# First image's attention: VectorE and ScalarE in written order, with the folding's work dealt out unit by unit

## The chip, the cores and the metric

The kernel runs on one core of a Trainium2 chip. The core has a matrix engine (TensorE, PE in the profile, its weight loads PEld), a vector engine (VectorE, DVE), an engine for activation functions (ScalarE, ACT), a general one (GpSimd, POOL) and an engine that issues transfers (SyncE, SP), each with its own in-order queue; they wait for one another through semaphores. The metric is the device time of one execution in microseconds, and the median of several executions is compared.

## The reference

Two layers follow each other on eight images of 512 channels and 32 x 32 positions.

```python
# layer 0, per image: group norm, q/k/v, each fake-quantized over ALL images, 8 heads of 64 channels
h = group_norm(xf, gn_w, gn_b)
qkv = einsum('oc,bct->bot', qkv_w, h) + qkv_b
q = fake_quant(q); k = fake_quant(k); v = fake_quant(v)
w = softmax(einsum('bct,bcs->bts', q * scale, k * scale))
a = einsum('bts,bcs->bct', w, v)
x = xf + einsum('oc,bct->bot', proj_w, a) + proj_b
# layer 1, per image: group norm, one head of 512 channels, no quantization
t = group_norm(x, gn_w, gn_b)
out = softmax((t wq + bq)(t wk + bk)^T / sqrt(C)) (t wv + bv)
x = x + (out wp + bp)
```

`fake_quant` needs the smallest and largest value of q, of k and of v over the whole batch, so no attention of layer 0 can start before all q, k and v exist.

## The kernel before, in words

**Stages.** The first stage normalizes all images, computes q, k and v, collects their extremes and stores them to DRAM (`q_d`, `k_d`, `v_d`). From about 585 us the scales are known and layer 0's attention begins. It is a generator, `attention()`, that is advanced four units at a time; with the second image on, layer 1 of the image before runs between its steps ("planned" part: `others()`).

**Units.** A unit `u` is one (image `b`, head pair `j`, half `hf` of the queries, key block `s` of eight). `scores(u)` puts two 64-row matmuls into one of two score buffers in PSUM (`st`); ScalarE takes the exponential into `pt` (four buffers) or, for every fourth unit of the first image (`plain`), into `aside`. `split(u)` makes a 16-bit high part of `pt` (a cast: on GpSimd for `s % 4 == 2`, on VectorE for `s == 5` before planning starts, on ScalarE otherwise) and VectorE subtracts to get the low part (`two<-pt,two`). `over_keys` multiplies both parts with v (`av`), `totals` with ones (`sm`). Eight units are a half, sixteen a pair, 64 an image. In one advance at unit u, the scores run up to nine units ahead and the splits with them. `finish` copies `av` and `sm` out of PSUM and starts the reciprocals of the row sums: two small loads (`apart`), `spread` on VectorE, a store and a broadcast load, then `divide`.

**Quantizing.** `load_pair(b, j, u)` is called sixteen units before a pair is used. It fetches the raw q and k (two buffers `raw`, which v shares), and `quants(i)` lists the steps `quant` and `quant2` for q, k, v (and `whole`, a 32-bit copy of part of v, in the first image).

**Folding.** Layer 1 uses folded weights, the product of two weight matrices (`wa` for q and k, `wm` for v and the output). `fold()` is a generator of 32 products and some small steps; nine steps are taken before attention starts, and then one in every second unit of the first image.

**What sets the order.** PE is always in written order (`mm` ties each matmul to the last one). VectorE and ScalarE are objects of the class `InOrder`. With `InOrder.planned` set (during the first image of stage one, and from the second image's first layer 1 on) each of their instructions is tied to the one before. Between, as in the first image's attention, a scheduler below the kernel chooses their order when the program is built. In that time the kernel has a list `dealt` of (unit, name, work): `deal(u)`, called by `split(u)`, takes the first entry whose unit has come, one per split, and `settle(name)` takes all of a name at once, as `scores` does with "qk" at the first unit of a pair and the main loop with "qv" when the pair's values are used. In the planned part `deal` isn't called, work goes through `dve.later` with times of the kernel's own planner, and `settle` still empties the list. Nearly all instructions go through line 91 (`call` in `InOrder`) or line 208 (`mm`), so the profile is read by the names of tiles.

Of the kernel before, what the change touches and what calls it, by code (L numbers as in the profile page):

```python
# [21 lines left out]
CC = C // P  # L22
# [36 lines left out]
def attn_pair_kernel(  # L59
# [12 lines left out]
    class InOrder:  # L72
# [1 line left out]

        planned = False

        def __init__(self, engine):
            self.engine, self.last, self.t, self.chores = engine, None, 0.0, []  # L80
# [6 lines left out]
        def __getattr__(self, name):  # L87
            op = getattr(self.engine, name)

            def call(*args, **kw):  # L90
                ins = self.latest = op(*args, **kw).ins  # L91
                if InOrder.planned:
                    if name == "dma_start":
                        self.t = max(self.t, pe.t) + 0.5
                    if self.last is not None:
                        tc.add_manual_dep(ins, self.last.name, IN_ORDER, reason="order")
                    self.last = ins
                elif self.last is not None:
                    tc.add_manual_dep(ins, self.last.name, IN_ORDER, reason="order")

            return call
# [204 lines left out]
    with ExitStack() as fast:  # L306
# [611 lines left out]
        def deal(u):  # L918
            i = next((i for i, (at, *_) in enumerate(dealt) if at <= u), None)
            if i is not None:  # L920
                dealt.pop(i)[2]()

        def settle(what):
            while True:
# [8 lines left out]
        def load_pair(b, j, u=None):  # L933

            nm = f"{b}_{j}"
            raws = []

            def fetch(i, src):
                if (b, j, i) == (0, 0, 2):
                    raw = aop.tile([P, NH, 512], F32, tag="ao", name="raw_first").rearrange(  # L940
                        "p h n -> p (h n)"
                    )
                else:
                    raw = raw_p.tile([P, T], F32, tag="raw", name=f"raw_{nm}_{i}")
                nc.sync.dma_start(
                    raw if i < 2 else raw.rearrange("p (t d) -> p t d", t=NT), src
                )
                raws.append(raw)

            def whole(raw, _, i):  # L950
                quant2(raw.rearrange("p (t d) -> p t d", t=NT)[:, 3::4, :], vfs[j], i)

            fetch(0, q_d[b][j])
            fetch(1, k_d[b][j])
            qt = qkp.tile([P, T], BF, tag="q", name=f"q_{nm}")
            kt = qkp.tile([P, T], BF, tag="k", name=f"k_{nm}")
            vt = qkp.tile([P, NT, P], F16, tag="v", name=f"v_{nm}")
            todo = (qt, kt, vt.rearrange("p t d -> p (t d)"))

            if b == 0:  # L960
                vfs[j] = xp.tile([P, 2, 256], F32, tag="x", name=f"vf_{nm}")[:, :, 0:P]

            def quants(i):
                for step in (quant, quant2, *([whole] if i == 2 and b == 0 else [])):
                    name, work = "qk" if i < 2 else "qv", lambda step=step: step(raws[i], todo[i], i)
                    if u is None or InOrder.planned:
                        dve.later(name, 0.7, work, pe.t + 12.0, 45.0)
                    else:
                        dealt.append((u + (10 if i < 2 else 18), name, work))

            def fetch_v():
                if len(raws) == 2:
                    fetch(2, v_d[b][:, :, bass.ts(j, P)])
                quants(2)

            if (b, j) == (0, 0):
                fetch(2, v_d[b][:, :, bass.ts(j, P)])
            quants(0)
            quants(1)
            if u is None or InOrder.planned:  # L980
                dve.later("qk", 0.0, fetch_v)
            else:
                dealt.append((u + 10, "qk", fetch_v))
            return qt, kt, vt


        def attention():
# [13 lines left out]
            def scores(u):  # L1001
                b, j, hf, s = units[u]
                if hf == 0 and s == 0:
                    settle("qk")
                nm = f"{b}_{j}_{hf}"
                qt, kt, _ = pairs[b, j]
                st = pair_ps(f"st_{nm}_{s}")
                if b == 0 and u % 2 == 1:
                    next(folding, None)
                awaits(st_free[-2])  # L1010
                for i, r in enumerate(HALF):
                    mm(
                        st[:, i, :], lhsT=kt[r, bass.ts(s, P)],
                        rhs=qt[r, bass.ts(hf, 512)], start=True, stop=True,
                    )
                if u >= 4:
                    need(u - 4)
                if plain(b, s):
                    pt = aside[:, u // 4 % 3].rearrange("p (i k) n -> p i (k n)", i=2)
                else:  # L1020
                    pt = ptp.tile([P, 2, 512], F32, tag="p", name=f"pt_{nm}_{s}")
                there = act.do(
                    1.12, lambda: act.activation(pt, st, AF.Exp, scale=esc),
                    max(pe.t + 0.25, ready.get(u - 4, 0.0) + 0.1),
                )
                st_free.append(there)
                pts[u] = pt, there
# [80 lines left out]
            def finish(b, j, hf, u):  # L1108
# [30 lines left out]
                def spread():  # L1139
                    r = rcs[:, n * 16 : (n + 1) * 16]  # L1140
                    dve.tensor_add(r, apart[:, 0, :], apart[:, 1, :])
                    dve.reciprocal(r, r)
                    nc.sync.dma_start(rs_d[n].rearrange("r (p k) -> (r p) k", k=16), r)
                    for i, r in enumerate(HALF):
                        nc.sync.dma_start(
                            rs[r], rs_d[n][2 * i : 2 * i + 2, :].partition_broadcast(CH)
                        )
                    if InOrder.planned:
                        dve.later("ao", elements(1100), divide, dve.t + 7.0, 20.0)
                    else:  # L1150
                        dealt.append((u + 17, "ao", divide))

                if InOrder.planned:
                    dve.later("ao", 0.4, spread, pe.t + 5.0, 8.0)
                else:
                    dealt.append((u + 10, "ao", spread))

            for u in (0, 2, 4):
                for i in (u, u + 1):
# [542 lines left out]
        def fold():  # L1702
# [16 lines left out]
            def through(i):  # L1719
                w, _, col = ((NQ1, NK1, V_BQ), (NV1, WP1, V_BV))[i]  # L1720
                z = small.tile([P, CC], F32, tag="z", name=f"z{i}")
                for e in range(CC):
                    dve.tensor_tensor_reduce(
                        room, wn[w][:, e, :], row, 1.0, 0.0, ALU.mult, ALU.add,
                        accum_out=z[:, e : e + 1],
                    )
                dve.tensor_add(z, z, vec[:, col : col + CC])
                widen(wide[:, i], z)

            for i, (rows, lw, rw) in enumerate(((wa_rows, NQ1, NK1), (wm_rows, NV1, WP1))):  # L1730
                for e in range(CC):
                    ps = bank(f"fold_{lw}_{e}")
                    for d in range(CC):
                        mm(
                            ps, lhsT=wn[lw][:, d, bass.ts(e, P)], rhs=wn[rw][:, d, :],
                            start=(d == 0), stop=(d == CC - 1),
                        )
                        if d + 1 < CC:
                            yield
                    act.copy(rows(e), ps.rearrange("p (a n) -> p a n", a=2))  # L1740
                    if e == CC - 1:
                        through(i)
                    yield
                dst, w = ((gb, NK1), (ob, WP1))[i]
                by_channel, _ = weigh(
                    bank, room, lambda e, w=w: wn[w][:, e, :], wide[:, i], f"f{i}"
# [3 lines left out]
                if i == 0:  # L1750
                    dve.tensor_copy(dst, tot)
                    a11, a12, a21, a22, s1, s2, s4 = (wa[:, i] for i in range(7))
                    tt(s1, a21, a22, ALU.add)
                    tt(s2, s1, a11, ALU.subtract)
                    tt(a21, a11, a21, ALU.subtract)
                    tt(s4, a12, s2, ALU.subtract)
                    yield
                    load_wp(0, nc.sync.dma_start)
                    load_x2(0, nc.sync.dma_start)
                else:  # L1760
                    dve.tensor_add(dst, tot, vec[:, V_BP : V_BP + CC])
            (m11, m12), (m21, m22), (v1, v2), (v3, v4) = ([t[:, i] for i in range(2)] for t in wm)
            tt(v1, m11, m12, ALU.subtract)
            tt(v2, m22, v1, ALU.subtract)
            tt(v3, m22, m12, ALU.add)
            tt(v4, m21, v2, ALU.subtract)
            for t, dst in zip(wm, wm_d):
                nc.sync.dma_start(dst, t)

        def check_sums():  # L1770

# [45 lines left out]
        folding = fold()  # L1817
        for _ in range(9):
            next(folding)
        while done < 1:  # L1820
            advance()
        for _ in folding:
# [1 line left out]

        for _ in range(LEAD):
            advance()
        for e in (dve, act):
            e.t = pe.t
        InOrder.planned = True
# [367 lines left out]
```

## Time and profile before

| | |
|---|---|
| median of three runs | 2587.91 us (2587.77 to 2590.59) |
| profiled execution | 2593.63 us, span 2591.8 us |
| first exponential of the first image | 591.34 us |
| first exponential of the second image | 701.39 us |
| first projection matmul (planned part) | 725.53 us |
| PE busy between 591.34 and 701.39 (110.05) | 101.61 us |
| DVE, ACT busy there | 97.84, 100.55 us |

A line of a timeline has the start, the time taken, the engine, the line, the operation, the tiles written and read, the number of instructions merged, and in brackets the idle time before it with what ended it. A line of a table by stretch has the stretch, its length, the busy time and number of instructions of PE, PEld, DVE, ACT and POOL, the granted PE clock (1.00 is full), and the share and speed of the DMA engines. The profiled execution is one run of its own; its times are compared with those of another profiled execution, and differences are put onto the median.

### The profile page before, as it was taken

How to read it: one execution, taken by the hardware profiler on the slowest of the kernel's cores; microseconds unless marked ns; L12 is line 12 of the kernel's file. 1: busy time of each engine (PE TensorE's matmuls, PEld its weight loads, DVE VectorE, ACT ScalarE, POOL GpSimd, SP SyncE). 2: the span in 40 equal slices, each digit the busy share in tenths (PEclk: the TensorE clock that was granted, in tenths of full speed). 3: DMA queues.
4: the chain of work that ended last, by engine and by line, in shares of the span. 5: the costliest groups of instructions: out<-in, count | busy, mean ns of one | idle time of the engine just before them, and what ended most of it. 6: DMA issues, size and time to landing. Idle time of an engine off the chain costs nothing.

```text
span 2591.8 us, 38710 instructions
## 1 busy us (share of the span) xinstructions
PE 2530.8 (98%) x15670; PEld 1756.9 (68%) x15670; DVE 1905.4 (74%) x2748; ACT 1358.8 (52%) x1696; POOL 195.6 (8%) x153
## 2 busy tenths in 40 slices
PE   7999999999889999999999999999999999999998
PEld 4788888873237765775677577757756775777787
DVE  6788777669867877777877787778777777775544
ACT  3222222218856675665566566747665665664121
POOL 0000000002210001000100010010001000100000
PEclk9899999999999999999999999999999999999999
DMA  4343333334311232223212331232232123212211
GB/s 168 130 146 136 114 120 121 130 124 137 115 50 54 62 115 98 62 79 111 86 58 73 121 99 58 95 112 65 79 107 99 46 79 122 83 54 82 86 37 39
DMA packets 156013, 243.09 MB, mean 94 GB/s; under 512 B 26544, under 2 KB 93104, under 8 KB 154288
## 3 DMA queue, kind: packets, MB, share of 16 engines
q1 hardware_dynamic: 125264, 182.81, 21.2%
q10 hardware_dynamic: 30560, 57.71, 6.5%
q8 instruction: 125, 2.05, 0.3%
q14 instruction: 64, 0.52, 0.1%
HBM read 153.64 MB, written 86.28 MB: 93 GB/s over the span
## 4 chain that ended last, share of the span: by engine, by line
PE 65%; DVE 3%; ACT 2%; issue 1%; DMA 1%; POOL 0%; ACTq 0%; SPq 0%; DVEq 0%
PE s L208 15%; PE o L208 14%; PE pj L208 9%; PE v2ps L208 7%; PE av L208 7%; PE g L208 6%; PE st L208 4%; PE sm L208 3%; ACT pt L91 1%; DVE acc L91 1%; DVE two L91 1%; DVE h L91 0%; DMA out_dram<-x 0%; DVE kept_u L91 0%; DVE p L91 0%
## 5 line engine op out<-in xcount | busy, mean ns | idle before, releaser
L91 ACT ACTIVATE pt<-st,esc 128x1024 f32<-128x1024 f32 x496 | 528.1, 1114 | 350.6 <-PE st L208 327.2
L91 DVE TENSOR_TENSOR two<-pt,two 128x1024 f16<-128x1024 f32 x496 | 603.9, 1233 | 131.0 <-POOL two L1047 107.3
L91 ACT CAST two<-pt 128x1024 f16<-128x1024 f32 x358 | 362.3, 1055 | 5.3 <-ACT p L91 5.1
L1047 POOL CAST two<-pt 128x1024 f16<-128x1024 f32 x128 | 173.2, 1353 | 1533.2 <-PE sm L208 768.5
L208 PE MATMUL av<-two,v 128*32 128x512 f16 x3968 | 245.8, 382 | 0.7 <-ACT ao L91 0.7
L208 PE MATMUL s<-g,h 128*128 128x256 f32 x1024 | 233.5, 381 | 0.0
L208 PE MATMUL pj<-ao,wp 128*128 128x512 f32 x512 | 223.6, 595 | 0.0
L208 PEld LDWEIGHTS s<-g,h 128*128 128x128 f32 x1024 | 193.4, 190 | 30.5 <-issue 4.3
L91 ACT ACTIVATE u_ring<-qkps,qkbt 128x512 f32<-128x512 f32 x89 | 61.0, 685 | 253.1 <-PE qkps L208 238.3
L208 PE MATMUL st<-q,k 64*128 64x512 bf16 x1024 | 166.6, 384 | 21.6 <-ACT pt L91 16.4
L208 PEld LDWEIGHTS <-v 128*32 128x32 f16 x3968 | 91.9, 96 | 134.4 <-issue 61.9
L208 PE MATMUL s<-g,sums 128*128 128x256 f32 x768 | 178.6, 382 | 0.2 <-DVE p L91 0.2
L208 PEld LDWEIGHTS pj<-ao,wp 128*128 128x128 f32 x512 | 96.3, 190 | 121.1 <-issue 110.9
L208 PE MATMUL o<-p,v 128*128 128x256 f32 x768 | 175.2, 382 | 1.0 <-DVE p L91 1.0
L208 PEld LDWEIGHTS o<-p,v 128*128 128x128 f32 x768 | 144.6, 190 | 26.8 <-issue 5.7
L208 PEld LDWEIGHTS s<-g,sums 128*128 128x128 f32 x768 | 144.8, 190 | 24.2 <-issue 4.1
L208 PEld LDWEIGHTS <-k 64*128 64x128 bf16 x1024 | 35.8, 94 | 159.8 <-issue 158.2
L208 PE MATMUL sm<-two,ones 128*32 128x512 f16 x1984 | 136.8, 381 | 0.0
L208 PE MATMUL qkps<-half,w_low 128*128 128x512 f32 x480 | 132.6, 399 | 1.9 <-DVE half L91 1.9
L208 PE MATMUL qkps<-half,w_high 128*128 128x512 f32 x480 | 134.4, 403 | 0.0
L208 PE MATMUL qkps<-half,w_mix 128*128 128x512 f32 x480 | 132.6, 399 | 0.6 <-DVE half L91 0.6
L208 PE MATMUL g<-h,wa 128*128 128x256 f32 x512 | 120.9, 385 | 1.8 <-DVE h L91 1.8
(221 smaller groups left out, 3832.1 us busy)
## 6 DMA issues: line engine op xcount, KB each, us to landing
rs<-rs_d SPq DMA_DIRECT2D x76, 256.0 KB
x<-in_x_dram SPq DMA_DIRECT2D x32, 512.0 KB
q_d<-wa SPq DMA_DIRECT2D x32, 512.0 KB
k_d<-wa SPq DMA_DIRECT2D x32, 512.0 KB
v_d<-v_ring SPq DMA_DIRECT2D x32, 512.0 KB
raw<-q_d SPq DMA_DIRECT2D x32, 512.0 KB
raw<-k_d SPq DMA_DIRECT2D x32, 512.0 KB
x_d<-h SPq DMA_DIRECT2D x64, 256.0 KB
```

The costliest lines, as they stand in the source:

```text
L91: ins = self.latest = op(*args, **kw).ins
L208: ins = nc.tensor.matmul(ps, lhsT=lhsT, rhs=rhs, **kw).ins
L1047: copy(two[:, 0], pt)
```

## The change

While the first image's attention is written, VectorE and ScalarE are now tied to the written order (`strict`, set after the first nine folding steps). With no scheduler to move work about, the other work of these engines is spread by hand through `dealt`: the row sums of folding (`through`, now started at the first product instead of the last), the sums for `wa` and `wm` and the stores of `wm` become entries that are taken one per split; q's steps are due at 12 and 13 units after the call of `load_pair`, k's at 14 and 15, v's at 19 and on (before: 10, 10 and 18); v's load follows q's second step directly (before: an entry of its own behind k); a pair's reciprocals are due at 12 instead of 10 units, its division at 20 instead of 17. Folding takes three steps in eight units instead of four, and goes on into the second image's first units.

```diff
-                if InOrder.planned:
                     if name == "dma_start":
                         self.t = max(self.t, pe.t) + 0.5
+                if InOrder.planned or InOrder.strict:
                     if self.last is not None:
                         tc.add_manual_dep(ins, self.last.name, IN_ORDER, reason="order")
...
         def deal(u):
             i = next((i for i, (at, *_) in enumerate(dealt) if at <= u), None)
             if i is not None:
                 dealt.pop(i)[2]()
+                if dealt[i : i + 1] and dealt[i][2].__name__ == "fetch_v":
+                    dealt.pop(i)[2]()
...
             def quants(i):
-                for step in (quant, quant2, *([whole] if i == 2 and b == 0 else [])):
+                for n, step in enumerate((quant, quant2, *([whole] if i == 2 and b == 0 else []))):
...
-                        dealt.append((u + (10 if i < 2 else 18), name, work))
+                        dealt.append((u + (12, 14, 19)[i] + n, name, work))
+                        if (i, n) == (0, 1):
+                            dealt.append((u + 13, "qk", fetch_v))
...
-            else:
-                dealt.append((u + 10, "qk", fetch_v))
...
-                if b == 0 and u % 2 == 1:
+                if u % 8 in (1, 4, 6):
                     next(folding, None)
...
-                        dealt.append((u + 17, "ao", divide))
+                        dealt.append((u + 20, "ao", divide))
...
-                    dealt.append((u + 10, "ao", spread))
+                    dealt.append((u + 12, "ao", spread))
...
                 for e in range(CC):
-                    dve.tensor_tensor_reduce(
+                    dealt.append((0, "fold", lambda e=e: dve.tensor_tensor_reduce(
...
-                dve.tensor_add(z, z, vec[:, col : col + CC])
-                widen(wide[:, i], z)
+                def last():
+                    dve.tensor_add(z, z, vec[:, col : col + CC])
+                    widen(wide[:, i], z)
+
+                dealt.append((0, "fold", last))
...
-                    if e == CC - 1:
+                    if e == 0:
                         through(i)
                     yield
+                settle("fold")
...
-                    tt(s1, a21, a22, ALU.add)
-                    tt(s2, s1, a11, ALU.subtract)
-                    tt(a21, a11, a21, ALU.subtract)
-                    tt(s4, a12, s2, ALU.subtract)
+                    for args in (
+                        (s1, a21, a22, ALU.add), (s2, s1, a11, ALU.subtract),
+                        (a21, a11, a21, ALU.subtract), (s4, a12, s2, ALU.subtract),
+                    ):
+                        dealt.append((0, "wa", lambda args=args: tt(*args)))
...
-            for t, dst in zip(wm, wm_d):
-                nc.sync.dma_start(dst, t)
+            def keep():
+                for t, dst in zip(wm, wm_d):
+                    nc.sync.dma_start(dst, t)
+
+            dealt.append((0, "wm", keep))
...
             next(folding)
+        InOrder.strict = True
         while done < 1:
             advance()
...
         for _ in range(LEAD):
             advance()
+        settle("wa")
+        settle("wm")
         for e in (dve, act):
             e.t = pe.t
         InOrder.planned = True
```

The four sums for `wm` become entries in the same way as those for `wa`.

## The prediction

> **What bounds the kernel now.** I read the page first, then busy time by stretch, the waits of the first image's attention, and there the instructions in order of time on TensorE (PE), ScalarE (ACT) and VectorE (DVE). The profiled execution took 2593.63 us (its span 2591.8, about 1.8 around it); the median of the runs is 2587.91, so I work out a difference on the trace and add it to the median. 0.2% is 5.2 us, about what a measurement of this kernel can tell from no change.
>
> ```profile
> PE 2530.8 (98%) x15670; PEld 1756.9 (68%) x15670; DVE 1905.4 (74%) x2748; ACT 1358.8 (52%) x1696; POOL 195.6 (8%) x153
> ```
>
> PE is 98% busy and runs its instructions in their written order, so the end moves by what PE waits, wherever it waits. I count units u = 0, 1, ...: one block of scores, one exponential on ACT each; eight are a half, sixteen a head pair, 64 the first image. Stretches of the first image (busy us of PE, weight loads, DVE, ACT, POOL, then the granted clock):
>
> ```profile
> 610.00:620.00 10.00, 10.00 (x100) 3.54 (x100) 9.96 (x11) 9.62 (x12) 1.81 (x2) 1.00 0.32 122
> ...
> 650.00:660.00 10.00, 8.21 (x72) 2.61 (x64) 7.00 (x10) 6.36 (x9) 1.44 (x2) 0.91 0.50 155
> ...
> 690.00:700.00 10.00, 8.20 (x104) 2.73 (x100) 8.64 (x10) 9.71 (x12) 1.55 (x1) 1.00 0.26 80
> ```
>
> While folding lasts (to about 683) PE is full, ACT has slack; afterwards ACT is full and PE idles a fifth. DVE is nearly full in the first row: three engines close to balance. The exponentials of units 8, 16 and 64, found by counting ACT's list:
>
> ```profile
> 603.60 1.11 ACT L91 ACTIVATE pt<-st,esc 128x1024 f32<-128x1024 f32 x1 [0.21 <-PE st L208]
> ...
> 617.25 1.11 ACT L91 ACTIVATE pt<-st,esc 128x1024 f32<-128x1024 f32 x1 [0.16 <-PE st L208]
> ...
> 701.39 1.17 ACT L91 ACTIVATE pt<-st,esc 128x1024 f32<-128x1024 f32 x1
> ```
>
> A half in the folding part takes 13.65 us; units 8 to 64 take 97.8 (13.97 a half, one DMA wait around 655 included).
>
> **Two rules weighed.** The Trainium skill, "SBUF — State Buffer", section "Who interferes with whom": a DVE instruction with two SBUF inputs and a GpSimd one that reads SBUF block each other. The trace agrees: POOL's cast at 629.16 ran inside the first subtraction below, which took 2.06 us against 1.21; I charge 0.84 per POOL cast.
>
> ```profile
> 629.68 2.06 DVE L91 TENSOR_TENSOR two<-pt,two 128x1024 f16<-128x1024 f32 x1
> 631.66 0.68 DVE L91 CAST two<-pt 128x1024 f16<-128x1024 f32 x1
> 632.52 1.21 DVE L91 TENSOR_TENSOR two<-pt,two 128x1024 f16<-128x1024 f32 x1
> 633.66 0.74 DVE L91 TENSOR_SCALAR raw<-raw,rcp 128x1024 f32<-128x1024 f32 x1
> ```
>
> "TensorE: Matmul & The Clock Gate", section "What's actually happening", has the clock halve after an idle window of about 3.4 us. Here a 1.79 us wait already did it: sixteen matmuls took 1.90 us instead of 1.05. I go by the trace: a PE wait of several us is followed by up to about 3.2 us at half speed.
>
> ```profile
> 658.01 0.51 PE L208 MATMUL st<-q,k 64*128 64x512 bf16 x2 [1.79 <-ACT pt L91]
> 658.48 1.90 PE L208 MATMUL av<-two,v 128*32 128x512 f16 x16
> ```
>
> **Part 1, folding spread evenly (PE).** Folding goes from every second unit to three in eight, so it lasts the whole image and costs 3 steps a half. PE per half, by start-to-start times: 8 score blocks x 0.32, 3 fold steps x 1.06, values and sums 1.42 + 1.51 + 1.42 + 2.46 = 12.55 us. ACT: 8 exponentials x 1.00, 3 casts x 0.95, 2 row copies and 0.75 fold copies x 0.48 = 12.2. So a half could run at 12.6; seven halves 88.2 instead of 97.8: a gain of 9.6. Unit 8 itself comes at about 603.1 (ACT from 591.34: eight exponentials, three casts and one copy, 11.3, and 0.45 for two casts and an exponential that follow on their own input), a gain of 0.5.
>
> **Part 2, DVE in written order: k is quantized just in time (PE waits).** Before, the order built for DVE has q and k of pair 1 ahead of the first subtraction and k of pair 2 after unit 14's, sixteen units before use; no score block of the first image but the very first waits for DVE. In the changed program q's two steps stand with units 12 and 13, k's with 14 and 15, k's second behind the subtraction of unit 14, and the weight load of k for the score blocks of units 16, 32, 48 and 64 carries a wait on DVE. PE can do nothing else meanwhile, ACT's next instruction is exponential 16, nothing covers it. The chain, from exponential 8 as zero: ACT does 8, 9, two casts, 10 to 13 (at 1.00 and 0.95: 7.85), two row copies (PE ends the sums they read at about 8.7), then unit 12's cast, ending near 10.0. From there DVE alone: subtraction 1.13, q 0.67, cast of unit 13 0.71, subtraction 1.13, first step of k 0.67, subtraction of unit 14 1.13, k 0.75 = 6.2, plus 0.84 for the POOL cast of unit 14, plus 0.1 of signalling: k at 17.1, scores 0.39, exponential 16 at 17.5. Against 12.6 that is a bubble of 4.9, four times: 19.6. Bounds: 3.0 if the cast comes a us earlier and POOL's cast falls in DVE's idle time; 6.0 if DVE is late into the half (the sums of wa, wm and the divisions add up to 2.4 in some). Half speed after a bubble: halving 3.2 us could cost 1.6; PE then has little slack, but part lies under ACT: I take 0.6 in each of the three halves that follow within the image, 1.8 (bounds 0 and 4.8).
> Sum: unit 64 at 603.1 + 88.2 + 19.6 + 1.8 = 712.7 instead of 701.39: +11.3.
>
> **Part 3, the other dealt work.** The row sums of the first weights (4 x 0.68 and 0.7 of small steps) leave the stage before and stand between subtractions of units 0 to 4, where DVE waits for casts: nothing. wa's and wm's sums (8 x 0.6), and divisions three units later: DVE has 2 us idle before unit 12's cast in most halves, nothing; without that cover the bubble above grows by them, which is its upper bound. SP's queue: the v loads come after q's second step, six units before use (before, DVE waited 2.2 us for one); the rows of reciprocals pass behind at most one 512 KB store of wm, with eight units for a round trip that took 6.1 us (694.2 to 700.3). Units 64 to the projection took 24.14; afterwards ACT's work there is 20.5 (12 exponentials, 7 casts, 4 copies) + 0.39 + 1.42, with 2 of waits and slow clock the same: nothing (bounds -2 and +2).
>
> **Part 4, what spills into the planned part.** The second step of k for pair 1 of the next image now follows the projection's fourth eviction (739.57): two steps end at 741.65, its scores began at 741.41: +0.3. v of that pair is dealt too late to come out before planning starts, and is emitted when unit 80 is begun: behind the four normalizations of h. Before, DVE did it at 757 (first fence, DVE's list) and PE went on at 763.95 (second, PE's):
>
> ```profile
> 757.05 0.70 DVE L91 TENSOR_SCALAR v<-raw,bhi 128x1024 f16<-128x1024 f32 x1
> ...
> 769.68 1.92 DVE L91 TENSOR_SCALAR h<-h,gmean_b,grstd_b 128x512 f32<-128x512 f32 x4
> ```
>
> ```profile
> 763.95 1.05 PE L208 MATMUL av<-two,v 128*32 128x512 f16 x16
> ...
> 770.27 3.75 PE L208 MATMUL g<-h,wa 128*128 128x256 f32 x16 [1.76 <-DVE h L91]
> 777.71 3.61 PE L208 MATMUL g<-sums,wa 128*128 128x256 f32 x8 [3.69 <-ACT two L91]
> ```
>
> Now v's two steps of 0.67 follow h (769.68 + 1.83): v is ready at 771.5 + 1.34 = 772.9; values, sums and scores of 3.5 us follow, the first product of h starts at 776.4 instead of 770.27, ends at 780.2; DVE then needs 1.3 for the sums of the next: 781.5 against 777.71, where PE had waited 3.69 anyway. That is +3.8; half speed after 9 us of waiting adds up to 1.7 (the old product there, 3.61 for eight, was slow as well): +4.5 taken.
>
> **Sum.** 11.3 + 0 + 0.3 + 4.5 = +16.1: 2609.7 for a profiled execution, 2604 for the median.
>
> **Rivals.** (a) Not slower: DVE runs far enough ahead that k is there when exponential 14 frees the score buffer, so only part 1 shows. Place: scores of 16, 32, 48, 64. Price: 10.1 gained, less 4.8 of part 4. It decides if a bubble is below (10.1 - 4.8) / 4 = 1.3 us; with none, 2582.6, with one that just evens out, no change. For it: DVE idles in every half before unit 12's cast. Against: the cast's place on ACT, behind exponential 13 and two copies, bounds the chain whatever DVE did earlier. Chance 0.13, split between faster and same.
> (b) Slower by more: each bubble also costs the half-speed 1.6 in full and a late DVE makes it 6: 603.1 + 88.2 + 24 + 4.8 = 720.1 (+18.7), part 4 +5.8, +1 in the tail: 2613. For it: the slow stretches at 658 and 709. Chance 0.2.
> (c) The spread folding gains as said and the bubbles are at their lower bound 3.0: 88.2 + 12 + 603.1 = 703.3 (+1.9) and part 4 at 4.1: +6, 2594. Chance 0.17.
> The forecast holds 0.5. Range 2592 to 2613, from (c) to (b). Slower by over 0.2%: 0.5 + 0.2 and nearly all of (c), 0.86; (a) and the rest of (c) leave 0.08 within 0.2% and 0.06 faster.
>
> **What would show it.** Waits of "PE st" (or its weight load) on DVE k, four of about 5 us, in the first image; PE lower, not fuller, in its stretches; folding to the end of it; exponential 64 near 713; a PE wait of 8 to 9 us before the values of unit 80, with DVE's v step right after the four h steps. The prediction is wrong if ACT reaches unit 12's cast well before 10 us into its half, since the whole chain hangs on that, or if a shared limit that I don't count keeps the halves between the bubbles at 13.65.

## The result, and the profile after

The changed kernel takes 2616.86 us (median of five runs, 2616.55 to 2618.87) against 2587.91 beside it: ratio 1.0107, 95% interval 1.0093 to 1.0121, or 28.95 us more. The forecast was 2604.0: slower, as said, but by nearly twice as much, and outside its range. The profiled execution of the changed kernel took 2616.86 us too (span 2615.1). That of the kernel before had a first stage some 4.6 us longer (first exponential at 591.34 against 586.76), so stages are compared here from the first exponential on, and totals by the medians.

Busy time, the page's first part; then the granted clock in 40 slices, in which slices 10 and 11 now hold an 8:

```profile
PE 2532.9 (97%) x15670; PEld 1749.2 (67%) x15670; DVE 1905.7 (73%) x2748; ACT 1360.2 (52%) x1696; POOL 189.2 (7%) x153
...
PEclk9999999998899999999999999999999999999999
```

TensorE has the same work. From the first exponential to the end of the last stage of the table below it is busy for 5.4 us more (172.41 and 177.84) in a stretch that is 28.45 us longer: most of what was added is waiting, and about a fifth is the same work done more slowly. Its waits over the execution (what it waited for, us in total, times, longest):

```profile
PE st L209 <- DVE k L91: 23.3, 5, 5.9
PE st L209 <- ACT pt L91: 9.7, 17, 1.7
PE av L209 <- DVE v L91: 9.5, 1, 9.5
...
PE pj L209 <- DVE ao L91: 2.0, 1, 2.0
```

Of these, only the second was there before. The exponentials of units 8, 16 and 64 on ScalarE, to be held against the three shown of before:

```profile
599.64 1.11 ACT L91 ACTIVATE pt<-st,esc 128x1024 f32<-128x1024 f32 x1 [0.98 <-PE st L209]
...
618.28 1.11 ACT L91 ACTIVATE pt<-st,esc 128x1024 f32<-128x1024 f32 x1 [5.70 <-PE st L209]
...
717.86 1.11 ACT L91 ACTIVATE pt<-st,esc 128x1024 f32<-128x1024 f32 x1 [5.71 <-PE st L209]
```

The half from 8 to 16 took 18.64 us against 13.65. Stage by stage, in us (a stage begins and ends with the event named):

| stage | before | forecast | after |
|---|---|---|---|
| exponential 0 to 8 | 12.26 | 11.8 | 12.88 |
| 8 to 64, seven halves | 97.79 | 109.6 | 118.22 |
| of these, four ending at the start of a pair (each) | 12.2 to 13.7 | 17.5 | 18.30 to 18.69 |
| the three between (each) | 13.64 to 17.17 | 13.2 | 14.46 to 15.15 |
| 64 to the projection | 24.14 | 24.1 | 23.90 |
| projection to the scores behind the first product of the sums | 60.90 | 65.7 | 68.54 |

The differences are 20.4 + 0.6 - 0.2 + 7.6 = 28.4; from there to the end both need the same (1805.4 and 1804.8 us).

The first of the four waits, on ScalarE, on VectorE and then on TensorE:

```profile
609.03 0.59 ACT L91 COPY rs<-sm 128x512 f32<-128x512 f32 x1 [0.47 <-PE sm L209]
609.51 1.05 ACT L91 CAST two<-pt 128x1024 f16<-128x1024 f32 x1
```

```profile
610.59 1.23 DVE L91 TENSOR_TENSOR two<-pt,two 128x1024 f16<-128x1024 f32 x1 [2.31 <-ACT two L91]
611.73 1.53 DVE L91 TENSOR_SCALAR q<-raw,bhi 128x1024 bf16<-128x1024 f32 x1
613.18 0.68 DVE L91 CAST two<-pt 128x1024 f16<-128x1024 f32 x1
613.89 1.23 DVE L91 TENSOR_TENSOR two<-pt,two 128x1024 f16<-128x1024 f32 x1
615.03 0.75 DVE L91 TENSOR_SCALAR raw<-raw,rcp 128x1024 f32<-128x1024 f32 x1
615.70 1.22 DVE L91 TENSOR_TENSOR two<-pt,two 128x1024 f16<-128x1024 f32 x1
616.83 0.75 DVE L91 TENSOR_SCALAR k<-raw,bhi 128x1024 bf16<-128x1024 f32 x1
```

```profile
611.35 0.61 PE L209 MATMUL sm<-two,ones 128*32 128x512 f16 x8
617.63 0.61 PE L209 MATMUL st<-q,k 64*128 64x512 bf16 x2 [5.68 <-DVE k L91]
618.17 2.07 PE L209 MATMUL fold<-wn_h 128*128 128x512 f32 x2
```

VectorE stands still for 2.31 us until unit 12's cast (the second line of ScalarE's) is there and then does the seven steps of the forecast's chain in 6.99 us (7.03 were reckoned), k last. TensorE has nothing else that it may do. Behind the wait it is slow: two score matmuls take 0.61 instead of 0.39, a folding step 2.07 instead of 1.12.

The spill into the planned part, VectorE's list and TensorE's:

```profile
789.20 1.91 DVE L91 TENSOR_SCALAR h<-h,gmean_b,grstd_b 128x512 f32<-128x512 f32 x4
791.03 0.75 DVE L91 TENSOR_SCALAR raw<-raw,rcp 128x1024 f32<-128x1024 f32 x1
791.81 0.75 DVE L91 TENSOR_SCALAR v<-raw,bhi 128x1024 f16<-128x1024 f32 x1
```

```profile
792.62 1.90 PE L209 MATMUL av<-two,v 128*32 128x512 f16 x16 [9.45 <-DVE v L91]
...
797.96 3.72 PE L209 MATMUL g<-h,wa 128*128 128x256 f32 x16
803.22 1.97 PE L209 MATMUL g<-sums,wa 128*128 128x256 f32 x8 [1.54 <-DVE sums L91]
```

v's steps stand right behind the four of h, as forecast.

### The profile page after: what moved, and what is told of

Its sections match the earlier page's. It is cut to its first block, busy times and chain, and to the rows that moved or that the text cites. A ratio compares the mean times of both kernels' runs of the same rounds, so it can differ in the third digit from the quotient of the medians.

```text
span 2615.1 us, 38713 instructions
## 1 busy us (share of the span) xinstructions
PE 2532.9 (97%) x15670; PEld 1749.2 (67%) x15670; DVE 1905.7 (73%) x2748; ACT 1360.2 (52%) x1696; POOL 189.2 (7%) x153
## 4 chain that ended last, share of the span: by engine, by line
PE 86%; DVE 5%; ACT 3%; issue 2%; DMA 1%; POOL 0%; SPq 0%; ACTq 0%; DVEq 0%
PE s L209 15%; PE o L209 14%; PE qkps L209 12%; PE pj L209 8%; PE av L209 8%; PE v2ps L209 7%; PE g L209 7%; PE vps L209 6%; PE st L209 4%; PE sm L209 4%; DVE two L91 2%; ACT pt L91 1%; PE fold L209 1%; ACT two L91 0%; DVE acc L91 0%
## 5 line engine op out<-in xcount | busy, mean ns | idle before, releaser
L91 DVE TENSOR_TENSOR two<-pt,two 128x1024 f16<-128x1024 f32 x496 | 597.1, 1217 | 166.6 <-POOL two L1050 108.4
L1050 POOL CAST two<-pt 128x1024 f16<-128x1024 f32 x128 | 166.7, 1302 | 1568.2 <-ACT pt L91 779.8
```

Of the source, the lines that this page charges most:

```text
L1050: copy(two[:, 0], pt)
```

## The experiments

What the result suggests: k's late place (four waits), TensorE's half speed behind them, and two waits in the planned part (one for v, whose steps spill into it, one for a division) make up the loss, less a gain from spreading the folding. Rivals: the written order as such; the new dealing or folding; VectorE's load. The median of the kernel before moved between 2587.7 and 2589.7 us from one group of runs to the next, so a difference between runs of different groups is uncertain by a us or two; ratios are to the kernel before in the same group, and stages are from the traces. In these traces the first exponential comes at 586.2 to 591.3 us; why was not looked for, and a total can hide or feign 2 or 3 us by it, which the stages do not.

**q and k two units earlier.** One line of the changed kernel (`fetch_v` stays tied to q's second step):

```diff
-                        dealt.append((u + (12, 14, 19)[i] + n, name, work))
+                        dealt.append((u + (10, 12, 19)[i] + n, name, work))
```

> The changed kernel with q and k dealt two units earlier (q at units 10 and 11, k at 12 and 13 of a pair); nothing else moved. Theory (k's second step stands behind the subtraction of unit 14): it now stands behind that of unit 12, whose end was 611.8 in the changed kernel's trace, so k is there near 612.6 where TensorE asks for it near 612.0. TensorE's waits for k fall from 23.3 us to under 4, the halves that hold them from 18.5 to 13 to 14 us, the halves after them from 14.7 to about 13.2: in all 22 to 28 us less, 2589 to 2595. Rival A (the written order itself costs the time, wherever k stands): a wait for VectorE of the same size comes up at another operand, and the gain is below 8 us, over 2609. Rival B (the half-speed clock after the waits is a thing of its own, not of the waits): the waits go but the halves after them stay at 14.7, about 2598.

Measured: 2597.14 us, 19.7 less than the changed kernel (21.2 if each is set against the kernel before beside it); ratio to before 1.0033 (1.0020 to 1.0046). Two of its five waits for k:

```profile
640.80 0.39 PE L209 MATMUL st<-q,k 64*128 64x512 bf16 x2 [2.35 <-DVE k L91]
...
668.96 0.39 PE L209 MATMUL st<-q,k 64*128 64x512 bf16 x2 [2.29 <-DVE k L91]
```

Units 8 to 64 took 98.45 us, 19.8 less. So two units in the places of q and k carry two thirds of what the change lost, and most of the half speed went with the waits (one of the seven halves still has it). It fell short of the forecast 22 because 7.7 us of waits for k were left (under 4 expected).

**One part alone, or all but one part.** The order alone, in the kernel before (`planned or strict` in `call` as in the change):

```diff
             next(folding)
+        InOrder.strict = True
         while done < 1:
```

> The kernel before with one part of the change alone: VectorE and ScalarE are tied to the written order from the first image on; folding and dealing as before (k's two steps at units 12 and 13 of a pair, folding at every second unit, its sums in one piece). Theory (place of k, not the order): k stands behind the subtraction of unit 12, waits for k stay under 2 us each, the total is 2583 to 2598. Rival A (the order itself): waits for VectorE at the start of each pair as in the changed kernel, 2605 or more.

The changed kernel without it:

```diff
-        InOrder.strict = True
```

> The changed kernel without its written order: dealing, divisions and folding as changed, VectorE and ScalarE left to the scheduler. Theory: the scheduler puts k ahead of the subtractions, no wait for k, so 20 to 28 us less than the changed kernel: 2589 to 2597; the wait for v in the second pair of the second image stays (about 4.7 us). Rival (the new places in the dealing or the three folding steps in eight bring the time by themselves): 2608 or more.

The folding alone, in the kernel before:

```diff
-                if b == 0 and u % 2 == 1:
+                if u % 8 in (1, 4, 6):
```

> The kernel before with one other part alone: folding advanced at units 1, 4 and 6 of eight instead of at every second one. Theory: the halves of the first image fall from 13.7 to about 13.0 us (the kernel without the written order had 12.7 to 13.0 in its first four), v is handled as before, so no new wait in the second image: 4 to 6 us less than the kernel before, 2583 to 2586. Rival (the spread gains nothing, what the kernel without the order gained came from the later dealing): within 1.5 us of the kernel before.

| kernel | us | ratio to before (95%) | units 8 to 64 | projection to scores |
|---|---|---|---|---|
| order alone | 2598.91 | 1.0038 (1.0025 to 1.0052) | 109.42 | 61.05 |
| change without order | 2590.03 | 1.0000 (0.9991 to 1.0009) | 93.28 | 65.84 |
| folding spread alone | 2585.39 | 0.9985 (0.9977 to 0.9993) | 93.03 | 60.80 |

The folding is a gain: 4.1 us on the medians beside it (2589.45), with halves of 12.7 to 13.0 us where it was forecast to make 12.6. Without the order, the change has no wait for k in the first image, and its gain of 4.5 us in the first image is eaten by the spill (4.9). The order alone costs 9.6 us: k, dealt at 12 and 13, waits little (4.9 us in all), but folding's row sums now stand in one piece before the vector that TensorE wants from them:

```profile
681.18 2.35 PE L209 MATMUL wt_f<-wn_v,wide 128*32 128x512 f32 x8 [4.47 <-DVE wide L91]
```

So the total is just above what the theory gave (2598), by a wait that it had not named, and the part of the change that deals these sums one by one does remove a wait that the order makes.

**The spill.** The left-over entries are handed to the planner as it starts:

```diff
         InOrder.planned = True
+        while dealt:
+            _, name, work = dealt.pop(0)
+            dve.later(name, 0.7, work, pe.t + 12.0, 45.0)
```

> The changed kernel with the dealt steps that are left when the planned part begins (k of the pair (1,1), its v) handed to the planner instead of kept until the pair begins. Theory: v's steps are planned ahead of the four normalizations of h, TensorE's wait of 9.5 us for v goes, the first g product is there 4 to 5 us earlier, total 2611 to 2613. Rival: the normalizations stand ahead of the subtractions too, and the wait moves to them: within 1 us of 2616.9.

Measured: 2613.23 us, 3.6 less (5.1 set against the kernel before beside each); the wait for v is gone, and the stage from the projection to the scores took 64.77 instead of 68.54, 3.8 less. It is still 3.9 above the kernel before, with the wait of 2.0 us for a division among it.

**The half speed.** Multiplications without use fill the waits; the score block overwrites them:

```diff
                 awaits(st_free[-2])
+                if u in (16, 32, 48, 64):
+                    for n in range(38):
+                        mm(st[:, 0, 0:P], lhsT=ones, rhs=ones, start=True, stop=True)
```

> The changed kernel with 38 extra multiplications of 128x128 fp32 (about 5 us, no result used: the score block overwrites them) put ahead of the score blocks of units 16, 32, 48 and 64, where TensorE waits 5.7 us for k. Theory (after such a wait TensorE runs some 3 us at half speed, which costs about 1.8 us in each of the halves behind it): the waits for k shrink to below 1.5 us, the halves behind them fall from 14.5 to about 12.8 us, 5 to 8 us less than the changed kernel, 2609 to 2612, although TensorE does more work. Rival (those halves are long because VectorE and ScalarE are behind): they stay at 14.5 and the total stays within 1.5 us of 2616.9, or above it.

Measured: 2621.61 us. The 38 took 8.75 us and pushed the scores back by 3; yet the halves behind them fell to 12.98, 12.98 and 13.30. With `range(24)`:

> As the run with 38 extra multiplications, which took 8.75 us and not 5 (0.23 us each), with 24 of them: 5.5 us, as long as the waits of 5.7 us that they stand in. Theory (half speed after the waits): the halves with the waits stay at 18.2 to 18.6 us, the halves behind them are at 13.0 as in the run with 38, so 5 to 6 us less than the changed kernel: 2610 to 2612. Rival: the halves behind fell there only because the longer stop let VectorE and ScalarE catch up; then they are back at 14.5 and the total is 2615 to 2618.

Measured: 2612.19 us, 4.7 less than the changed kernel with more work on TensorE. By stretch (length, busy time and number of instructions of PE, PEld, DVE, ACT, POOL, clock), a half with the wait and the one behind it, of the changed kernel:

```profile
599.60:618.30 18.70, 12.86 (x119) 3.85 (x119) 12.85 (x13) 12.22 (x14) 2.35 (x2) 0.94 0.10 29
618.30:632.70 14.40, 14.40 (x131) 4.89 (x132) 6.82 (x7) 13.12 (x15) 1.99 (x2) 0.84 0.47 163
```

and with the waits filled:

```profile
601.75:620.18 18.43, 18.14 (x167) 9.22 (x168) 13.53 (x13) 12.21 (x13) 2.46 (x3) 1.00 0.10 29
620.18:633.17 12.99, 12.47 (x131) 4.58 (x132) 6.88 (x7) 12.96 (x15) 2.09 (x2) 1.00 0.58 204
```

VectorE and ScalarE come as late as before; only the clock differs, 1.00 for 0.84, and the second half is 1.4 us shorter. In units 8 to 64 the filling is worth 118.22 - 112.55 = 5.7 us: the price of the half speed there. Behind the fourth wait, from unit 64 to the projection, the filled kernel is 1.0 us faster as well (22.90 for 23.90).

**Everything mended, with and without the order.** q and k at 8 to 11, left-over entries to the planner (as above), divisions ahead of the list:

```diff
-                        dealt.append((u + (12, 14, 19)[i] + n, name, work))
+                        dealt.append((u + (8, 10, 19)[i] + n, name, work))
...
-                        dealt.append((u + 20, "ao", divide))
+                        dealt.insert(0, (u + 17, "ao", divide))
...
-                    dealt.append((u + 12, "ao", spread))
+                    dealt.insert(0, (u + 10, "ao", spread))
```

> The changed kernel, written order kept, with q and k dealt four units earlier (8 to 11), the left-over steps handed to the planner, and the divisions dealt ahead of everything else at the old distances (10 and 17). Theory (all of the loss is these three waits): against the kernel with k two units earlier (2597.1) the 7.7 us left of waits for k go, and with them 6 to 8 us, the wait for v (about 4 us) and that of the second half of the projection (2 us): 2581 to 2586. Rival (something of the written order remains that no wait shows): 2590 or more.

Beside it, the same mends of spill and divisions with q and k as in the change, and without the order:

> The changed kernel without the written order (2590.0) and with the left-over steps handed to the planner and the divisions ahead as in the run beside it. Theory: only the wait for v was left there: 4 to 6 us less, 2584 to 2586. Rival: the places of the divisions make a new wait in the first image, 2588 or more.

Measured: 2591.14 us (0.9998, 0.9990 to 1.0007) with the order, 2584.46 (0.9980, 0.9970 to 0.9990) without: the second beats both kernels, the first missed its 2586. Its halves were 12.5 to 13.2 us but for two; the worst, 18.28 us, held a new wait of 3.9 us for v of the third pair, behind folding's sums. Two more tries to get rid of such waits:

```diff
-            i = next((i for i, (at, *_) in enumerate(dealt) if at <= u), None)
+            due = [i for i, (at, *_) in enumerate(dealt) if at <= u]
+            i = next((i for i in due if dealt[i][0]), due[0] if due else None)
...
-                        dealt.insert(0, (u + 17, "ao", divide))
+                        dealt.insert(0, (u + 15, "ao", divide))
```

> As the run with q and k four units earlier (2591.1, where TensorE waited 3.9 us for v of the third pair, whose steps stood behind folding's sums in the dealing, and 2.0 us for the division of the last pair): steps of q, k, v and the divisions are now dealt before folding's sums, the division two units earlier. Theory: both waits go, with the half speed behind them; 7 to 10 us less: 2581 to 2584, below the kernel before and below the two kernels without the written order (2585.4 and 2584.5). Rival: folding's sums, now late, hold up TensorE's own product with them: 2587 or more.

Then v at 14 to 16, reciprocals at 9, divisions at 14, and `wm`'s sums left to the planner:

> As the run with everything mended (2592.9), in which TensorE still waited 3.5 us for v of the third pair (VectorE had three of folding's sums ahead of it), 2.7 us for the eviction of a projected block behind folding's last combinations, and 0.9 us for a division: v's three steps are dealt five units earlier (14 to 16), the division one unit earlier, and folding's last combinations are left to the planner. Theory (the written order costs nothing where each step stands early enough): those three waits go, with the half speed behind them: 7 to 10 us less, 2582 to 2586, as the kernels without the written order. Rival (VectorE is too full in these halves for any written order): a new wait for VectorE takes their place, 2589 or more.

Measured: 2592.90 (1.0014, 1.0007 to 1.0021) and 2594.69 us (1.0020, 1.0012 to 1.0028); the totals of the rivals, and in the second case the rival's mechanism too. Over all the stages of the table, from the first exponential on, their traces take 196.0 and 198.4 us, against 195.1 before and 190.0 for the kernel without the order. The waits move from operand to operand: 3.5 us for v and 2.7 for an eviction in the first, 3.0 for the eviction and again 5.2 for k in the second:

```profile
PE st L209 <- DVE k L91: 5.2, 2, 3.1
```

The first of these two kernels again, but with q and k as in the change:

> The changed kernel with the mends of the run beside it, but q and k dealt as in the change (12 to 15). Theory: against the run with v planned alone (2613.2) the wait of 2.0 us for the division goes, 2609 to 2612; what is left over the run beside it, 26 to 30 us, is k's late place alone. Rival: most of the loss isn't k's place: 2604 or less.

Measured: 2616.11 us, 0.75 less than the change. From the projection to the scores it gained 4.7 us, as meant, but the divisions, now ahead of k, made two of the halves that wait for k 1.3 and 0.6 us longer, and units 8 to 64 took 120.25. A miss of the expectation, and one more sign that what stands before k is paid in full. Against the run at 2592.90, from which it differs in the places of q and k alone, it is 23.2 us slower (26 to 30 were expected): most of the loss is k's late place.

**VectorE's load or its order.** The last kernel but for folding's work on VectorE, which is left out (row sums over 8 columns, combinations replaced by zero fills):

```diff
-                        room, wn[w][:, e, :], row, 1.0, 0.0, ALU.mult, ALU.add,
+                        room[:, 0:8], wn[w][:, e, 0:8], row[:, 0:8], 1.0, 0.0, ALU.mult, ALU.add,
...
-                        dealt.append((0, "wa", lambda args=args: tt(*args)))
+                        if args[0] is not a21:
+                            nc.gpsimd.memset(args[0], 0.0)
```

(and `wm` likewise), in the kernel with k and v earlier, and in the change itself:

> The run with k and v earlier (2594.7; waits of 3.1 and 2.2 us for k, 3.0 for an eviction) with folding's work on VectorE left out: the row sums take 8 columns instead of 512 and the combinations of wa and wm are replaced by zero fills on GpSimd, some 9 us of VectorE's time in the first image (its folded weights are wrong). Theory (VectorE is too full for a written order): the waits for k and for the eviction shrink to below 1 us each, 6 to 10 us less, 2585 to 2589. Rival (the order alone, by which step stands behind which wait): k's waits stay at 2 to 3 us, 2592 or more.

> The changed kernel with the same work on VectorE left out. Theory (the waits for k hang on the place of unit 12's cast on ScalarE and on VectorE's seven steps behind it, not on VectorE's load): the four waits stay at 5 to 6 us, the total is 2613 to 2617. Rival (VectorE's load makes them): they fall below 4 us, the total below 2609.

Measured: 2585.13 us, 9.6 less, and 2617.62, 0.8 more. Waits for k of the first:

```profile
PE st L209 <- DVE k L91: 2.3, 2, 2.0
```

One wait of 2.0 us for k was left, where under 1 was expected; the second and the one for the eviction went. A half of the kernel with everything mended (2592.9) suggests why the load matters there:

```profile
627.00:640.00 13.00, 12.47 (x119) 3.79 (x118) 12.93 (x17) 12.31 (x15) 3.31 (x3) 1.00 0.42 126
```

PE 12.5, ACT 12.3 and DVE 12.9 of 13.0: a VectorE that is bound to an order has hardly a gap left in which to catch up. Whether the kernel without the order would gain from the lighter load as well was not run, so how much of the 9.6 us belongs to the order stays open. In the change itself the same relief does nothing for k (its waits for k are 23.5 us in all, units 8 to 64 take 118.13): VectorE idles 2.3 us in front of unit 12's cast, and the wait hangs on what stands between that cast and k. Its planned part did gain: from the projection to the scores it took 65.81 instead of 68.54, and the wait for the division fell from 2.0 to 0.4. The total does not show it, since the first exponential came 2.2 us later (588.94 against 586.76).

## Why the prediction was wrong

- **Part 1, the folding: right in sign, half in size.** 9.6 us were forecast for the seven halves; alone it gave 4.8 in the trace (97.79 to 93.03; one half of the trace before had a stall of 3.5) and 4.1 in the medians. The bound of a half is 12.7 to 13.0, not 12.6, and two halves stayed at 14.0 and 14.7. Unit 8 came 12.88 after exponential 0, not 11.8; the cause of these 1.1 us stays open.
- **Part 2, the waits for k: right mechanism, right chain, two terms too small.** The four waits are where they were said to be. VectorE's chain was right to 0.04 us. Its start was not: unit 12's cast ended at 10.9 us of the half, not 10.0, since ScalarE's copy of the sums waited for TensorE (until 609.03, 9.4 us into the half, where 8.7 had been reckoned) and the cast stands behind it. With the waits filled, these halves take 18.3 us against 17.5: 3.3 us over four.
- **The failed step: "I take 0.6 in each of the three halves", 1.8 us.** It is the largest of the terms that were mis-sized: the run with the waits filled gives 5.7. The reason given, "part lies under ACT", does not hold: behind the wait all engines start late together, and TensorE was busy for the whole 14.40 us. Nor does the length: 3.2 us of half speed had been taken from the trace before, where a slow stretch of the first image lasts 3.41 us (658.16 to 661.57), but each of the four waits brought twice that, 6.83 us, which begins inside the wait. By stretch (length, busy time and number of instructions of TensorE, clock, then DMA), at the first wait:

```profile
615.97:622.80 6.83, 5.17 (x22) 0.50 0.34 107
```

Of the 6.83 us, 5.2, 6.1 and 3.2 fell on work behind the first three waits, and the three halves behind them lost 1.5, 2.2 and 1.2. That the sum, 4.8, is the forecast's upper bound is chance, since that bound was three times half of 3.2. The four halves with the waits lost 0.9 more, which was left out.
- **The halves between, clock apart:** 13.1 us against 12.6, 1.5 over three, near the 12.7 to 13.0 of the folding alone; what holds them above 12.6 was not found.
- **Part 3, "nothing": wrong by 2.** 64 to the projection was right (23.90). The later division was not free: TensorE waited 1.95 us for it in the second half of the projection, behind the sums of `wm` (0.4 us where folding's sums are left out).
- **Part 4, the spill: right, about a us too large in the change itself.** +4.8 was forecast for k and v. Handing v to the planner saved 3.8 us of that stage in the change, beside the wait for the division, and 4.8 in the pair of runs without the order (65.84 and 61.01).

Summed up: 3.3 + 3.9 + 1.5 in units 8 to 64 (8.6 in the trace), 1.1 before, 2.8 in the planned part, 0.2 the other way: 12.3 of the 12.9 us between 16.1 and 28.95. Rival (b) had the right idea, half speed in full, and with 24 for the waits, 4.8 for the clock and 5.8 for the spill was 4 us short.

## What to carry to other kernels

When an engine is tied to a written order, find for each operand of the full engine the instruction just ahead of its producer and ask what that one waits for: here two units in the places of q and k were worth 20 us, while relieving the producing engine of 9 us of work did nothing for the same waits. A wait of the matrix engine costs its length and the slow stretch behind it; filling it with work whose result nobody reads is a cheap way to measure the second part. Where three engines are within 6% of full, as in the halves shown here, each mend of a hand-written order moved the wait to the next operand until the producer was given some slack.

## What was not expected of the hardware

- **A wait of 2.3 us may or may not halve the clock.** In the run with k two units earlier, the half behind a wait of 2.35 us ran at a clock of 1.00 (13.15 us), the half behind one of 2.29 us at 0.88 (14.60 us). Behind 5.7 us it was always low (0.84, 0.82, 0.91). The Trainium skill, "TensorE: Matmul & The Clock Gate", section "What's actually happening", says that the window of about 3.4 us is free-running; the traces show something like it. In every trace here, each change of the granted clock comes a whole multiple of 3.41 us after the one before it, as on a grid. By steps of that grid, the two waits:

```profile
636.18:639.59 3.41, 2.27 (x29) 1.00 0.18 50
639.59:643.00 3.41, 2.19 (x18) 1.00 0.72 221
...
666.90:670.31 3.41, 1.35 (x4) 1.00 0.68 177
670.31:673.72 3.41, 3.41 (x23) 0.50 0.40 139
```

The first wait is split by a step of the grid, with 1.1 and 1.2 us without work on either side; the second lies almost whole in one step, with 2.1 us, and the next step is at half speed. The 1.79 us wait of the forecast lies in one step too (654.75 to 658.16). Over all 16 traces, from 585 to 830 us, every step at full clock with more than 2.01 us without work was followed by half speed, and none with less than 1.70. So a wait of this length can cost a slow stretch or none, depending on where it falls.
- **The extra multiplications cost what their columns say.** Each is two instructions of 128x128 fp32 in the trace: 76 took 8.75 us, 0.115 each. A folding step, one multiplication, is two of 128x512 and takes 1.06, 0.53 each: a quarter of the columns for 0.22 of the time. The 5 us expected for 38 were too few.
- **GpSimd's cast slows steps with one input too.** q's second step took 1.53 us beside the cast at 611.64, 0.74 without it (607.59 in the run with k earlier). The forecast charged 0.84 to a subtraction; the price was nearly the same (0.79), the victim another. (The cast at 629.16 did not run inside that subtraction, as the forecast has it: it took 1.50 us and had begun 0.52 us ahead of it.) The page and section named in the forecast, "SBUF — State Buffer", "Who interferes with whom", have this case too: `tensor_scalar` is listed there among the operations that can block against GpSimd, depending on their operands.
